# A list scheduler in the kernel's source takes over the order of every engine

## The chip, the cores and the metric

The kernel runs on one core of a Trainium2 chip. The metric is the device time of one execution in microseconds (us); several runs are taken and their median is compared. Lower is better. The engines that matter are TensorE (PE: matrix products and transposes into eight PSUM banks), VectorE (DVE), ScalarE (ACT), GpSimd (POOL), and SP, whose queue issues all of the kernel's DMAs. Each engine executes its own instructions in order, and they wait for each other through semaphores.

## The reference

Four layers are applied in turn to an activation `x` of 8 batches x 256 tokens x 512 features in fp32, with a conditioning vector `cond_2048` (8 x 512).

```python
# layer 0: conditioned RMS norm, 8 query heads on one key head (64 wide), SwiGLU MLP of 2048
h = ada_rms(x, t, ln1_w, ln1_tw); q, k = apply_rope(h @ Wq.T), apply_rope(h @ Wk.T); v = h @ Wv.T
x = x + softmax(q k^T / 8) v @ Wo.T
h = ada_rms(x, t, ln2_w, ln2_tw); x = x + (silu(h @ Wg.T) * (h @ Wu.T)) @ Wd.T
# layer 1: 16 heads of 32 with normalised q and k, a bias on the scores, gelu MLP of 2048, gates
x = x + attn(_ln(x) * (scale1 + 1) + shift1) * gamma1
x = x + (gelu_tanh((_ln(x) * (scale2 + 1) + shift2) @ Wfc1.T + bfc1) @ Wfc2.T + bfc2) * gamma2
# layer 2: 16 query heads on 4 key heads of 32, low-rank keys and values, a sparse causal mask
c_kv = h @ Wkd.T; k, v = c_kv @ Wku.T, c_kv @ Wvu.T
x = x + softmax(mask(rope(q) rope(k)^T / sqrt(32))) v @ Wo.T
# layer 3: 8 block experts of 64 -> 256 -> 64, layer norm with conditioning, silu, projection
y = gelu(xr @ W1 + b1) @ W2 + b2
x = x + silu(layernorm(y) * (1 + scale) + shift) @ out_W + out_b
```

## The kernel before

Tokens lie in 16 tiles of 128 x 512, which stay in SBUF from start to end (`x0` to `x15`), two to a batch. The stages follow each other: layer 0's attention, its MLP, layer 1's attention, its MLP, layer 2's attention, layer 3.

**Attention** (`attend`, three times). For each batch and group of four heads TensorE makes the scores into the four PSUM banks with the tag A (`scored`, L697, tiles of 32 or 64 rows). VectorE finds row maxima in A (L727; in layers 1 and 2 a custom operation that also adds a bias or mask, L743), and ACT takes Exp with row sums (L747). The probabilities are then turned with the tokens of the keys on the partitions: some by TensorE (`turned`, L783) and a copy by DVE or ACT (`copy`, L480 and L483), some by a DVE transpose of 32 x 32 blocks and a round trip through memory (four DMAs out, L549, and one back, L756: the tensors `flip`). The values are multiplied in (`weighted`, L808), the result is divided by the row sums (`divided`, L830; inverse sums go through memory as `spread`, L765 and L770), and the projection with `wo` is added to `x` (`added`, L631). The product helper L631 also makes queries, keys and values of the next batch, which `rope` (L649, L650) turns before they are transposed (L1258, L1264). Norms use statistics (L449, L450), a power on POOL, and a scaling (L468, L470); a batch's normalised tiles are transposed on TensorE (L500) or through memory (`turn`).

**MLPs** (`mlp`): products of 128 x 128 blocks, seven in place of eight by sums of blocks (Strassen), into C banks (L1024) and A banks (L1073).

**Conditions**: `cond_rows` and `modulation` (L316, L334) make scales and shifts from `cond_2048` and weights such as `wada1`.

What sets the order. `Program` calls the engines' methods through a tile framework in a given program order. Extra work (projection of the next batch, output of the last one, conditions) is kept in generators on `self.queue` and taken up between the steps of the attention by a credit of microseconds (`some`). The framework takes these instructions, tracks which tile each reads and writes, and puts them on the engines by a scheduler and cost model of its own; it also hands out the buffers of each tag (`BUFS`: four A banks, four C banks, four `p`, two `hT`, eight `wbig` and so on). Three hints in the source bend it: `tc.keep_in_program_order(...)` on modulations, on some products of values and on layer 2's first scores, and `tc.issue_after(self.last_dma)`, which queues the loads of the next layer behind the last inverse sums on SP.

Of the kernel before, what the change touches and what calls it, by code (L numbers as in the profile page):

```python
# [14 lines left out]

# [19 lines left out]
P = 128  # L35
# [3 lines left out]
KC = D // P  # L39
# [139 lines left out]

class Program:  # L180
    def __init__(self, ctx, tc, d, out):
        self.ctx, self.tc, self.nc, self.d, self.out = ctx, tc, tc.nc, d, out
        self.n = 0
        self.queue, self.credit = [], 0.0
        self.ready, self.calls = {}, 0

    def pool(self, name, psum=False):
        return self.ctx.enter_context(
            self.tc.tile_pool(
                name=name, bufs=1, reuse_waits="tile", **({"space": PSUM} if psum else {})  # L190
            )
        )

    def t(self, shape, tag, bufs=None, dtype=F32, pool=None):
        self.n += 1
        bufs = bufs or BUFS.get(tag)
        kw = {} if bufs is None else {"bufs": bufs}
        pool = pool or (
            self.psum if tag in "AC" else self.wbigp if tag == "wbig" else self.work
        )  # L200
        return pool.tile(list(shape), dtype, tag=tag, name=f"{tag}_{self.n}", **kw)
# [29 lines left out]
    def setup(self):  # L231
        nc, d = self.nc, self.d
        self.const = self.pool("const")
        self.xp = self.pool("xp")
        self.wqkvp = self.pool("wqkvp")
        self.wop = self.pool("wop")
        self.wbigp = self.pool("wbigp")
        self.work = self.pool("work")
        self.psum = self.pool("psum", psum=True)

        def c(shape, tag, **kw):
            return self.t(shape, tag, pool=self.const, **kw)
# [6 lines left out]
        self.x = [self.t([P, D], f"x{i}", pool=self.xp) for i in range(NT)]  # L249
# [11 lines left out]
        make_identity(nc, self.ident)  # L261
# [3 lines left out]
        for t in self.inv:  # L265
            nc.gpsimd.memset(t, 0.0)
        self.spread = [
            self.tc.dram_tile([32, P], F32, name=f"spread{i}") for i in range(4)
        ]
        self.n_spread = 0  # L270
        self.turns = [self.tc.dram_tile([P, KC * S], F32, name=f"turn{i}") for i in range(3)]
        self.n_turn = 0
        self.flips = [self.tc.dram_tile([P, 8 * P], F32, name=f"flip{i}") for i in range(4)]
# [94 lines left out]
    def ada_1(self):  # L368
# [11 lines left out]
        self.gammas = self.tc.dram_tile([2, B, D], F32, name="gammas")  # L380
# [202 lines left out]
    def modulate(self):  # L583

        for (name, b), entry in self.ready.items():
            hT, rows, kept, at, done = entry
            if rows is None and not done and at < math.inf:
                place, placed, _ = self.places(name, b, hT)
                for c in range(KC):
                    self.tc.keep_in_program_order(placed(c, c, place[:, c]))  # L590
# [64 lines left out]
    def attend(self, name, n_groups, hd, project, value, finish, work, key_tiles=(2, 2), biased=None,  # L655
# [29 lines left out]
        def scored(b, g):  # L685
# [3 lines left out]
            for j0 in range(0, 4, rows):  # L689
                for q in range(TB):  # L690
                    for j in range(j0, j0 + rows):
# [5 lines left out]
                        mm = nc.tensor.matmul(  # L697
# [3 lines left out]

                        if name == "attention2" and j == q == 0:
                            self.tc.keep_in_program_order(mm)
            return s

        def softmax(s, b):
# [61 lines left out]
            for c in range(nch):  # L768
                t = inverse[(self.n_spread * nch + c) % 4]
                dma = nc.sync.dma_start(  # L770
                    t, rows[c * per : (c + 1) * per, :].unsqueeze(1).to_broadcast([per, hd, S])
                )
                self.last_dma = dma.ins
# [16 lines left out]
        def weighted(b, g, pT):  # L790
# [11 lines left out]
            for c in range(nch):  # L802
                for k in range(TB):
                    mine = [n for n, (kk, q) in enumerate(pairs) if kk == k]
                    q0 = pairs[mine[0]][1]
                    for i in range(per):
                        j = c * per + i
                        mm = nc.tensor.matmul(  # L808
# [7 lines left out]
                        if j < self.in_blocks(name, b):  # L816
                            self.tc.keep_in_program_order(mm)
# [186 lines left out]
    def mlp_begin(self, name):  # L1004
        self.kept = self.tc.dram_tile([B, P, 7 * S], F32, name=name)
        self.first = self.blocked(0, self.hT)
# [213 lines left out]
    def layer0_begin(self):  # L1220
        nc = self.nc
        w = self.t([P, KC, 1536], "wqkv", pool=self.wqkvp)
        self.load(w[:, :, 0:512], "wq0T")
        self.load(w[:, :, 512:640], "wkv0T")
        wo = self.t([P, KC, D], "wo", pool=self.wop)
# [130 lines left out]
    def layer0_mlp(self):  # L1356
# [4 lines left out]
        spare = self.t([P, 4, 2, S], "wo", pool=self.wop)  # L1361
# [10 lines left out]
        with self.tc.issue_after(self.last_dma):  # L1372
            for i, tag in enumerate(("qT", "kT", "v", "qT")):
                load_down(i, tag)
            early = []
            for i, tag in ((4, "kT"), (5, "v")):
                early.append(self.t([P, 4, S], tag))
# [622 lines left out]
```

## Time and profile before

| What | Value |
|---|---|
| median of three runs | 2079.61 us (2076.65 to 2082.24) |
| the profiled execution: its span, first to last instruction | 2076.6 us, the profile's only time for it |
| mean granted TensorE clock | 0.987 |
| PE busy | 2006.0 us, 12818 matmul records |
| DVE, ACT, POOL busy | 1365.2, 748.1, 334.0 us |
| DMA | 208.91 MB, mean 101 GB/s |

The share of busy time is an average over stages with different limits. The stages in the span are: layer 0's begin and attention from 0 to 282 us, its MLP to 868, layer 1's attention to 1258, its MLP to 1650, layer 2's attention to 1935, and layer 3. A matmul's record shows its time from start to a modelled end, and records overlap; from the start of one to the start of the next is what it costs TensorE.

The profile names engines PE, PEld (loading of weights), DVE, ACT, POOL, SP; "L631" is a line of the kernel. A group `C<-wqkv,hT 128*128 128x512` writes a tile C from tiles wqkv and hT, with a matmul tile of 128 rows x 128 columns of the array and a moving operand of 128 x 512. What stands after `<-` in brackets is the engine, tile and line that ended an idle time.

### The profile page before, as it was taken

The numbers are of one execution on the slowest core, as the hardware profiler recorded it, in microseconds if no ns is written. First come the engines' busy times: TensorE is split into PE (matmuls) and PEld (weight loads), VectorE is DVE, ScalarE is ACT, GpSimd is POOL, SyncE is SP. The second block draws the span as 40 slices with busy tenths as digits, with TensorE's granted clock in tenths as the row PEclk, the third lists the DMA queues.
The fourth block names the chain that finished last, engine by engine and source line by source line (L and its number), as shares of the span: only waits on it lengthen the run. The fifth ranks groups of instructions, "written<-read, shape, count | busy, mean of one in ns | idle before, by whom it ended". The sixth has DMA issues, their size and how long they took to land.

```text
span 2076.6 us, 36333 instructions
## 1 busy us (share of the span) xinstructions
PE 2006.0 (97%) x12818; PEld 1480.9 (71%) x12818; DVE 1365.2 (66%) x4429; ACT 748.1 (36%) x2332; POOL 334.0 (16%) x372
## 2 busy tenths in 40 slices
PE   7999999999999999999999999999999989989999
PEld 4555579999999999954544447999999854445454
DVE  6867766656675555656676766776765678776544
ACT  4333421111111111136565653222222256565644
POOL 1111200000000000054544531000000021101411
PEclk9999999999999999999999999999999989999999
DMA  8543361112130010334555543233211245653411
GB/s 306 166 119 90 102 215 48 65 42 64 61 110 26 17 31 16 96 99 129 131 143 141 141 123 115 89 101 116 87 60 48 67 113 137 158 145 97 126 40 42
DMA packets 223685, 208.91 MB, mean 101 GB/s; under 512 B 83536, under 2 KB 184976, under 8 KB 223120
## 3 DMA queue, kind: packets, MB, share of 16 engines
q1 hardware_dynamic: 223504, 206.59, 34.3%
q8 instruction: 102, 1.67, 0.3%
q14 instruction: 79, 0.65, 0.1%
HBM read 135.46 MB, written 71.07 MB: 99 GB/s over the span
## 4 chain that ended last, share of the span: by engine, by line
PE 78%; DVE 7%; ACT 7%; DMA 4%; issue 2%; POOL 2%; SPq 1%; DVEq 0%; ACTq 0%; POOLq 0%
PE C L1024 29%; PE A L1073 18%; PE C L631 17%; PE A L697 3%; ACT p L747 3%; PE C L808 3%; ACT wbig L747 2%; PE C L783 2%; PE C L1887 2%; PE A L1789 1%; DMA turn<-hT 1%; PE C L1822 1%; DVE st L449 1%; DMA wbig<-in_wgT 1%; DVE n L650 1%
## 5 line engine op out<-in xcount | busy, mean ns | idle before, releaser
L1024 PE MATMUL C<-hT,wbig 128*128 128x128 f32 x3072 | 416.4, 275 | 0.0
L1024 PEld LDWEIGHTS C<-hT,wbig 128*128 128x128 f32 x3072 | 388.8, 192 | 9.0 <-issue 2.4
L631 PE MATMUL C<-wqkv,hT 128*128 128x512 f32 (+1 forms) x768 | 316.6, 553 | 0.9 <-ACT v L1516 0.4
L1073 PE MATMUL A<-wbig,p 128*128 128x256 f32 x1024 | 242.2, 379 | 0.0
L631 PEld LDWEIGHTS C<-wqkv,hT 128*128 128x128 f32 x768 | 134.0, 195 | 122.8 <-issue 108.5
L1073 PEld LDWEIGHTS A<-wbig,p 128*128 128x128 f32 x1024 | 189.7, 190 | 23.1
L1054 DVE TENSOR_TENSOR p<-p,C 128x256 f32<-128x256 f32 x192 | 79.3, 421 | 162.5 <-PE C L1024 160.8
L1044 ACT COPY p<-C 128x128 f32<-128x128 f32 x192 | 51.3, 267 | 370.3 <-PE C L1024 361.8
L1024 PE MATMUL C<-qk,wbig 128*128 128x128 f32 x1152 | 160.0, 275 | 0.0
L1024 PE MATMUL C<-ctxT,wbig 128*128 128x128 f32 x1152 | 160.0, 275 | 0.0
L457 POOL TENSOR_SCALAR r<-mv 128x2 f32<-128x2 f32 (+1 forms) x28 | 7.1, 254 | 929.0 <-DVE mv L450 929.0
L747 ACT ACTIVATE p<-p,low 128x256 f32<-128x256 f32 x256 | 127.3, 501 | 69.9 <-DVE low L743 48.4
L1024 PEld LDWEIGHTS C<-qk,wbig 128*128 128x128 f32 x1152 | 144.1, 192 | 0.0
L1024 PEld LDWEIGHTS C<-ctxT,wbig 128*128 128x128 f32 x1152 | 144.1, 192 | 0.0
L747 ACT ACTIVATE wbig<-wbig,low 128x128 f32<-128x128 f32 (+1 forms) x256 | 113.7, 448 | 78.9 <-DVE low L743 75.9
L1398 ACT ACTIVATE p<-C 128x128 f32<-128x128 f32 x64 | 17.8, 278 | 294.9 <-DVE p L1054 294.9
L1045 DVE TENSOR_TENSOR p<-p,C 128x128 f32<-128x128 f32 x192 | 55.0, 286 | 97.5 <-ACT p L1044 96.4
L631 PE MATMUL C<-wo,ctxT 128*128 128x512 f32 x224 | 103.1, 600 | 1.2 <-DVE ctxT L830 1.2
L1504 POOL TENSOR_TENSOR ss<-ss,neg_half 128x16 f32<-128x16 f32 x32 | 93.8, 2931 | 2.7
L747 ACT ACTIVATE p<-A,low 128x256 f32<-128x256 f32 x128 | 59.3, 486 | 87.0 <-DVE low L727 75.9
L697 PE MATMUL A<-kT,qT 32*128 32x256 f32 (+2 forms) x896 | 85.9, 399 | 1.4 <-ACT p L747 0.6
L697 PEld LDWEIGHTS A<-kT,qT 32*128 32x128 f32 (+1 forms) x896 | 52.4, 191 | 41.9 <-issue 29.0
(268 smaller groups left out, 3507.6 us busy)
## 6 DMA issues: line engine op xcount, KB each, us to landing
flip<-p SPq DMA_DIRECT2D x160, 128.0 KB
p<-flip SPq DMA_DIRECT2D x40, 512.0 KB
turn<-hT SPq DMA_DIRECT2D x120, 128.0 KB
flip<-wbig SPq DMA_DIRECT2D x112, 96.0 KB
wbig<-flip SPq DMA_DIRECT2D x28, 384.0 KB
hT<-turn SPq DMA_DIRECT2D x16, 512.0 KB
kept<-hT SPq DMA_DIRECT2D x16, 512.0 KB
hT<-kept SPq DMA_DIRECT2D x16, 512.0 KB
```

What stands on the lines that cost most here:

```text
L631: self.nc.tensor.matmul(out, lhsT(k), rhs(k), start=(k == 0), stop=(k == n - 1))
L697: mm = nc.tensor.matmul(s[j][:, at[q] : at[q] + wide[q]], lhsT(q), keys, start=True, stop=True,)
L747: nc.scalar.activation(out, src, AF.Exp, bias=low[:, q : q + 1], scale=sign, accum_out=tot[:, j, q : q + 1],)
L783: nc.tensor.transpose(m[:, n * P : (n + 1) * P], p[:, at[q] + k * P : at[q] + (k + 1) * P], self.ident,)
L808: mm = nc.tensor.matmul(o[i * hd : (i + 1) * hd, c * S + q0 * P : (c + 1) * S], value(got[b][1], g, j, k), weights(j, mine), start=(k == 0 ...
L1024: nc.tensor.matmul(m[:, c : c + P], w[:, k * P : (k + 1) * P], b[:, k], start=(first and k == 0), stop=(k == steps - 1), skip_group_check= ...
L1044: nc.scalar.copy(g[:, 0, :], m[:, 0:P])
L1045: nc.vector.tensor_tensor(g[:, 0, :], g[:, 0, :], m[:, P : 2 * P], ALU.add)
L1054: nc.vector.tensor_tensor(g[:, 1:3, :], g[:, 0, :].unsqueeze(1).to_broadcast([P, 2, P]), m[:, 2 * P : 4 * P].rearrange("p (i t) -> p i t", ...
L1073: nc.tensor.matmul(acc[at][:, half * S : (half + 1) * S], left, right, start=(p == 0 and half == 0), stop=(p == 3), skip_group_check=True,)
L1504: nc.gpsimd.tensor_tensor(r, r, self.neg_half[:, 0:16], ALU.pow)
L1887: nc.tensor.matmul(m[:, half * S : half * S + S], left[:, r, i, :], right[:, i, :], start=(first and i == 0), stop=(i == 1), skip_group_ch ...
```

## The change

The program is no longer handed to the framework as it is made. `Program` gets a `Recording` in place of `nc`: `rec.tensor`, `rec.vector`, `rec.scalar`, `rec.gpsimd` and `rec.sync` note each call as an `Op` with its engine, outputs and inputs, and tiles are stand-ins without a place. `Scheduler` then

- builds the graph of dependencies by exact regions of tiles (`graph`), with whole banks for the tags A and C,
- walks the recorded operations once in order, with the buffer counts of each tag, and gives every operation a place (`program_order`),
- and goes through time (`run`): at each step it takes the engine that can start the earliest. On that engine it looks at up to 40 operations whose predecessors have been issued (`choice`), works out when each could start, and takes the one that comes first in place among those that start within 5 ns of the earliest, 200 ns on TensorE. A tile gets its buffer at its first use, if the tiles that come later in place still fit (`room`, `safe`).

Times come from formulas in the source: `duration` for DVE, ACT and POOL, `transfer` for DMAs, and the class `Tensor` for TensorE, with the change of tile shape, the overlap of tiles on different parts of the array, and table loads on ACT.

`Recording.issue` then issues the operations in that order, and adds a dependency without semaphore from each to the one before it on its engine, so that the framework keeps it. All tiles are allocated once, as homes by tag and slot; the framework still sets the semaphores. The pools, `keep_in_program_order` and `issue_after` are gone. The calls that make up the computation are the same. The diff, cut to its core:

```diff
+class Unit:
+    def __getattr__(self, method):
+        def issue(*args, **kwargs):
+            self.rec.ops.append(Op(ENGINES[self.name], self.name, method, args, kwargs))
+        return issue
...
+class Recording:
+    def issue(self, ctx, tc, order):
+        nc = tc.nc
+        seq, slots = order
...
+        make_identity(nc, real(self.ident))
+        info = mybir.DependencyInfo(mybir.DependencyClass.NoSync, mybir.DependencyReason.DATA)
+        before = {}
+        for i in seq:
+            op = self.ops[i]
+            done = getattr(getattr(nc, op.unit), op.name)(
+                *[real(a) for a in op.args], **{k: real(v) for k, v in op.kwargs.items()}
+            ).ins
+            if op.engine in before:
+                tc.add_manual_dep(done, before[op.engine], info, reason="order")
+            before[op.engine] = done.name
+LATENCY = {"PE": 38, "DVE": 33, "ACT": 33, "POOL": 35, "SP": 60}
...
+class Tensor:
+    def place(self, form, t):
+        mode, part, turn, _ = form
+        first = 84 if mode != (P, P) else 55 if turn else 104
+        if mode != self.mode:
+            return max(t, self.end + 94), first
+        soon = max(self.parts.get(part, 0.0), self.last + 7)
+        t = max(t, soon)
+        return t, first if t > soon + 30 and t > self.end + 20 else 0
...
+class Scheduler:
+    WINDOW, NEAR, NEAR_PE = 40, 5, 200
...
+        def choice(e):
+            found = []
+            for at, i in waiting[e]:
+                r = room(i)
+                if r is None:
+                    continue
+                t = max(free[e], ready[i], r + LATENCY[e] if r > 0 else 0.0)
+                extra = 0
+                if e == "PE":
+                    t, extra = pe.place(cost[i], t)
+                elif e == "ACT" and cost[i][2] not in (None, table):
+                    extra = 1283
+                found.append((t, extra, at, i))
+                if len(found) >= self.WINDOW:
+                    break
+            if not found:
+                return None
+            near = min(t + extra for t, extra, _, _ in found)
+            near += self.NEAR_PE if e == "PE" else self.NEAR
+            t, extra, _, i = min((f for f in found if f[0] + f[1] <= near), key=lambda f: f[2])
+            return t, extra, i
...
+            if e == "PE":
+                end = pe.put(cost[i], t, extra)
+                free[e] = t
+            elif e == "SP":
+                landed = max(t + 1690, landed) + cost[i]
+                free[e], end = t + 360, landed + 450
+            else:
+                took, busy, needs = cost[i]
+                free[e], end = t + extra + busy, t + extra + took
...
-        pool = pool or (
-            self.psum if tag in "AC" else self.wbigp if tag == "wbig" else self.work
-        )
-        return pool.tile(list(shape), dtype, tag=tag, name=f"{tag}_{self.n}", **kw)
+        return self.nc.tile(list(shape), dtype, tag, f"{tag}_{self.n}", bufs or BUFS.get(tag, 1))
...
-                    self.tc.keep_in_program_order(placed(c, c, place[:, c]))
+                    placed(c, c, place[:, c])
...
-        with self.tc.issue_after(self.last_dma):
-            for i, tag in enumerate(("qT", "kT", "v", "qT")):
-                load_down(i, tag)
...
+        for i, tag in enumerate(("qT", "kT", "v", "qT")):
+            load_down(i, tag)
...
+    rec = Recording()
+    Program(rec, d, out).run()
+    order = Scheduler(rec).run()
     with tile.TileContext(nc) as tc:
         with ExitStack() as ctx:
-            Program(ctx, tc, d, out).run()
+            rec.issue(ctx, tc, order)
```

The order that results, as both programs show it: in layer 1 and layer 2 many groups of scores stand ahead of the value products that came before them; at the start two groups' Exp stand together on ACT, with the angles' Sin behind them; the statistics of layer 2's second batch and one of its normalised tiles stand in the tail of layer 1's MLP on VectorE.

## The prediction

> **What bounds the kernel now.** I read the page first, then the time cut by stage, then the chain, then TensorE's waits, then two stretches in order of time. The page's busy times:
>
> ```profile
> PE 2006.0 (97%) x12818; PEld 1480.9 (71%) x12818; DVE 1365.2 (66%) x4429; ACT 748.1 (36%) x2332; POOL 334.0 (16%) x372
> ```
>
> TensorE binds, but 97% hides room, since a record's time holds its waits and its pipeline. The chain in order of time (start us, us, what) gives the true pitch:
>
> ```profile
> 315.33 3.02 PE A L1073 x14
> 318.36 6.25 PE C L1024 x56
> ...
> 2059.10 13.75 PE C L631 x32
> ```
>
> So a 128-column matmul record costs 6.25/56 = 0.112 us, 256 columns 3.02/14 = 0.216, 512 columns 0.430. From start to start in the trace, a 512-column record followed by one of another tile shape takes 0.522 instead of 0.429: a change of shape costs 0.093. Matmuls on different 32-row, 32-column or 64-wide parts start 0.007 apart and overlap. I laid all 7,002 matmul instructions of the kernel's order (12,818 records: two passes each, 1,186 transposes one) end to end at these pitches, with its 406 changes of shape: 1919.0 us. The span is 2076.6, so **157.6 us are stalls**. By stage (columns: stretch, length, busy of PE, PEld, DVE, ACT, POOL, clock, DMA share, GB/s):
>
> ```profile
> 0.00:100.00 100.00, 82.04 (x440) 47.83 (x442) 71.72 (x227) 36.76 (x101) 15.65 (x37) 0.93 0.72 239
> ...
> 282.00:868.00 586.00, 586.00 (x4406) 559.71 (x4403) 362.36 (x1175) 95.36 (x285) 6.53 (x14) 1.00 0.20 61
> ...
> 868.00:950.00 82.00, 80.34 (x354) 45.90 (x353) 51.61 (x161) 32.89 (x97) 40.77 (x34) 0.94 0.38 105
> ...
> 950.00:1200.00 250.00, 248.78 (x1374) 121.74 (x1369) 170.88 (x571) 150.68 (x477) 132.78 (x115) 1.00 0.54 142
> ...
> 1650.00:1710.00 60.00, 50.58 (x270) 32.47 (x268) 42.54 (x167) 27.49 (x98) 16.67 (x18) 0.86 0.35 91
> ...
> 1710.00:1935.00 225.00, 203.29 (x1458) 107.64 (x1458) 169.93 (x722) 136.83 (x529) 41.91 (x49) 0.98 0.51 131
> ```
>
> Span less end-to-end time per stage: layer 0's start and attention (0 to 282 us) 50, its MLP -1, layer 1's attention (868 to 1258) 36, its MLP -1, layer 2's attention (1650 to 1935) 59, layer 3 and the tail 15. The two MLPs (978 us) can give nothing. Of the 158, idle gaps are 2076.6 - 2006.0 = 70.6, and a granted clock of 0.987 over the span costs 0.013 x 2076.6 = 27; the other 60 lie inside records. TensorE's longest waits (us in total, times, longest):
>
> ```profile
> PE C L316 <- DMA condT<-in_condT: 6.8, 1, 6.8
> ...
> PE C L631 <- issue: 5.8, 3, 1.9
> ...
> PE C L500 <- DVE n L470: 5.3, 2, 3.2
> ...
> PE C L334 <- DVE n L330: 3.4, 1, 3.4
> ```
>
> The first is the first load and stays. The others are single places where something was queued in an unlucky order.
>
> **The change, part by part.** Both programs have the same 7,002 matmuls, 4,429 VectorE operations (same kinds and counts) and 1,073 DMAs; only order and buffer places differ. The stages stay apart: laid end to end, the first score of layer 2 comes at 1583.9 us in the old order and 1579.8 in the new, so nothing of an MLP moves into an attention stage, and gains must come from the 158.
>
> *Packing.* The new order has 384 changes of shape, 22 fewer: 22 x 0.093 = 2.0. Laid end to end it is 1915.4: **-3.6** (ends -4 and -3, since this is counted).
>
> *Tables on ACT at the start.* The old order alternates Exp and Sin:
>
> ```profile
> 33.12 1.28 ACT L1215 ACT_TABLE_LOAD   x1
> ...
> 34.84 1.28 ACT L747 ACT_TABLE_LOAD   x1
> ...
> 36.72 1.28 ACT L1217 ACT_TABLE_LOAD   x1
> ...
> 38.52 1.28 ACT L747 ACT_TABLE_LOAD   x1
> ```
>
> The new order runs all eight Exp of two groups before the next Sin. Table loads go from 22 to 16: four fewer here (5.1 us of ACT), two fewer where layer 0's MLP begins, worth nothing because TensorE is 100% busy there and nothing of it waits. The loads at 38.52 end in a 2.08 us gap of TensorE at 40.44, and the clock is 0.5 from 41.1 to 47.9 (3.4 us lost). I take **-4**; ends 0 (the transposes wait for VectorE's reductions instead) and -8.5 (all 5.1 and the clock).
>
> *Conditions at the start.* The second product of layer 1's conditions has its transposes some 28 rows of scores and transposes later in the new order, where the old one has three scores between. That covers the 3.4 us wait (L334) and its half clock, 3.4 us at 0.5, 1.7 lost: up to -5.1. New wait: the first product now stands ahead of the first scores, right behind the transposes that ran at 24.3 us, so the rest of the first transposes and the scores behind it would wait for two 1 MB loads of wada1. About 6.3 MB are issued up to them; at the 311 GB/s moved from 24 to 48 us that is 20.3 us, beside a first use at about 25. Cover 4 us, gone if the loads share the rate with the 5 MB behind them: +5. I take **-4**; ends -5.1 and +5.
>
> *SP's queue.* The old order held later loads behind the last spread of the attention. Now wada2 (1 MB) and three blocks of wdT (1.5 MB) are issued ahead of the first spread: 2.5 MB/311 GB/s = 8.0 us later for the inverse sums. Behind them wait VectorE's division (L830), then the product with wo; in the old trace that wait was 1.2 us in all, and the new order has two batches' transposes and the condition products in front. I take **0**; ends 0 and +8. The four parts of a flip now interleave with the next group's; each is one SP issue of about 0.4 us, and SP waits 36.5 us for flips already without TensorE waiting more than 2.4 us for them. Other start and attention waits of layer 0 (50 less those named): **-2**, ends -5 and +5.
>
> *Layer 2's beginning* (start us, us, engine, line; idle before):
>
> ```profile
> 1668.22 2.59 PE L697 MATMUL A<-kT,qT 32*128 32x128 f32 x16
> 1672.90 0.69 PE L500 MATMUL C<-ident,n 128*128 128x128 f32 x2 [2.10 <-DVE n L470]
> 1676.76 1.54 PE L500 MATMUL C<-ident,n 128*128 128x128 f32 x6 [3.16 <-DVE n L470]
> ```
>
> The old order puts batch 1's statistics and both normalised tiles behind the first group's softmax on VectorE. The new one has the statistics and the first tile in the MLP's tail, where VectorE has gaps, and puts ten further scores ahead of the second tile's first transpose. The 5.3 us go; the clock at 0.5 from 1672.6 to 1682.9 (5.1 lost) may go with them. Next late is the softmax itself. I take **-8**; ends -10.4 and +3 (its A banks are not read in time).
>
> *Scores ahead of their predecessors' products.* Counting complete groups of value products (L808) behind each group of scores, scores lead by 1.97 groups in layer 1 and 2.91 in layer 2 before; 2.75 and 3.22 after (about 25 and 10 of 32 groups move by one). In layer 2 a group of value products is 0.86 us, so VectorE's reductions start that much sooner; 1710 to 1935 has some 42 us of stalls, three of them the 1.9 us gaps shown as issue. 10 groups x 0.86 = 8.6. I take **-8**; ends -22 (half of the 42) and +10. In layer 1, 950 to 1200 is 99.5% busy with 14 us of stalls in six batches, so there is little to win; a score that comes before its bank A is read now holds the products behind it. I take **+2** there and **-5** for the stage's two ends (12 and 10 us of stalls), together **-3**; ends -15 and +15.
>
> At layer 1's beginning the clock is 0.50 from 911.5 to 921.7 although TensorE was busy 3.48 of the 3.50 us before it, in a run of 32-row scores; the new order keeps that run. So by the rows the 5.1 us lost there stay. The Trainium skill, "TensorE: Matmul & The Clock Gate", Part 1 (the HAM clock gate), puts a return to half rate down to an idle window of about 3.4 us; by that rule the stretch before 911.5 would not have triggered it, and an order without gaps would win all of it. By the rule the sum would be some 5 us lower; I go by the row.
>
> *Layer 3.* Its table loads stay (Gelu and Silu still alternate), the order differs little: **0**; ends -3 and +4.
>
> Sum: -3.6 - 4 - 4 + 0 - 2 - 8 - 8 - 3 + 0 = -32.6, so a span of 2044. The profiled span, 2076.6, is 3.0 below the median of the three runs (2079.6); the same distance puts the new median at **2047 us** (-1.6%).
>
> **Rivals.**
> *Early scores block TensorE (slower).* TensorE takes its order strictly. A group of scores needs its four A banks, which VectorE empties in eight reductions at about 0.5 us each (0.42 and 0.08): 4.0 us. Counting work of TensorE between a wait and the newest matmul it depends on, 184 waits now have under 1.5 us of cover, against 154 before. If each of the 35 moved groups waits 1.9 us more (half the reductions), that is +67 and the time 2114. It decides from 0.9 us per group (33/35). For: that count. Against: VectorE is 63 to 76% busy in these stages.
> *The order changes nothing that matters (no change).* Stalls are chains of ACT and VectorE whose lengths stay, and each gap reappears one group on: only packing and half of the table term remain, 2079.6 - 3.6 - 2 = 2074. Against: the named gaps have one cause each.
> *Loads crowd the start.* The new waits for wada1 and the spread come to +13 in place of -4: 2064.
> *Most stalls of attention go.* Half of layers 1 and 2 (48), 12 at the start, 3.6 packing: 2016.
>
> **How the numbers follow.** Forecast 0.47, most stalls go 0.15, loads crowd 0.07, no change 0.08, blocking 0.23. The forecast's own range is 2025 to 2066. For 8 in 10, the low end reaches past the strong case to 2008 (with the tables' end of -8.5 too), the high end to 2098, half-way into blocking. About 0.3% (6 us) is what a measurement tells from none: faster takes the first three, 0.69; no change gives 0.07 to same and 0.01 to slower, which with blocking is 0.24.
>
> **What would show it.** Right: two table loads fewer around 33 to 40 us and no 2 us gap there; no 3 us gap at layer 2's first L500 transposes; mean clock above 0.99; PE busy plus gaps near 2044; the MLPs unchanged at 586 and 392. Wrong: new gaps before the scores (A banks) released by VectorE, layer 1's attention longer than 390 us, or a first condition product waiting for wada1.

## The result: 0.7% slower, and where the time went

The changed kernel takes 2094.0 us (median of 4 runs, 2090.9 to 2099.5), beside 2080.4 for the kernel before (4 runs): a ratio of 1.0071, 95% interval 1.0053 to 1.009. The profiled span is 2092.7 us; before it was 2076.6, so 16.1 us more have to be found. The forecast was 2047, faster. The direction was wrong; the time lies near the slow end of the stated range (2008 to 2098).

The page of the changed kernel, its line of busy times:

```profile
PE 1995.5 (95%) x12818; PEld 1486.6 (71%) x12818; DVE 1410.0 (67%) x4429; ACT 742.9 (36%) x2326; POOL 332.4 (16%) x372
```

TensorE's records are 10.5 us shorter, its gaps 26.6 longer (97.2 in place of 70.6). By stage (stretch, length, busy of PE, PEld, DVE, ACT, POOL, clock, DMA share, GB/s):

```profile
0.00:100.00 100.00, 77.60 (x451) 44.20 (x452) 81.45 (x248) 32.37 (x99) 19.20 (x42) 0.98 0.78 260
282.00:868.00 586.00, 584.61 (x4366) 552.88 (x4365) 378.84 (x1153) 94.82 (x293) 6.50 (x14) 1.00 0.18 54
868.00:950.00 82.00, 81.73 (x417) 55.50 (x416) 58.92 (x177) 28.54 (x78) 32.00 (x29) 1.00 0.45 121
950.00:1200.00 250.00, 244.40 (x1384) 123.11 (x1383) 173.11 (x573) 153.79 (x489) 132.79 (x114) 1.00 0.52 139
1650.00:1710.00 60.00, 58.62 (x299) 40.97 (x297) 45.69 (x164) 27.00 (x93) 14.69 (x16) 0.91 0.40 99
1710.00:1935.00 225.00, 199.20 (x1420) 107.84 (x1420) 169.14 (x728) 132.75 (x516) 27.47 (x35) 0.95 0.52 133
```

Layer 1's beginning now runs at full clock. (From layer 1 on, the changed kernel's stages lie some 16 us later than those of the kernel before, so rows of the same times do not hold quite the same work.) The waits of TensorE (us in total, times, longest) say what was paid for it. All operations now have line 320, so one goes by tiles; `kept_flip` is the tensor `flip` of the kernel before, `kept_spread` is `spread`, `kept_turn` is `turn`:

```profile
PE C L320 <- DMA p<-kept_flip: 33.9, 11, 10.3
PE C L320 <- DMA wbig<-kept_flip: 15.6, 9, 3.2
PE C L320 <- ACT wbig L320: 8.1, 8, 4.1
PE C L320 <- DMA condT<-in_condT: 6.9, 1, 6.9
PE C L320 <- DVE n L320: 4.5, 7, 1.7
...
PE A L320 <- ACT p L320: 0.4, 1, 0.4
```

The first two lines are value products that wait for the read-back of a flip: 49.5 us, where the kernel before had 2.4. 22.9 of them are four waits between 100 and 282 us. The last line is what the strongest rival stood on, scores blocked by a bank A: 0.4 us.

The prediction's ledger (the order laid end to end at the trace's pitches, and the rest as stalls), in us. Each layer's column ends at the layer's last value product and begins where the column before it ends, so it holds the MLP that comes before its attention; "rest" is what follows layer 2's last value product, layer 3 above all:

| kernel | end to end | layer 0 | layer 1 | layer 2 | rest | span |
|---|---|---|---|---|---|---|
| before | 1919.0 | 49.8 | 34.2 | 58.9 | 14.7 | 2076.6 |
| changed | 1915.4 | 69.7 | 30.6 | 58.6 | 18.4 | 2092.7 |
| difference | -3.6 | +19.9 | -3.6 | -0.3 | +3.7 | +16.1 |

So the loss is layer 0's, and layer 2's gain is missing. SyncE's queue in time (start us, us, what) shows how layer 0 came about. The kernel before, one group:

```profile
174.32 1.76 SPq L549 DMA_DIRECT2D flip<-p  x4
176.18 0.56 SPq L765 DMA_DIRECT2D spread<-invT  x1
178.09 0.34 SPq L756 DMA_DIRECT2D p<-flip  x1
178.52 1.07 SPq L770 DMA_DIRECT2D wqkv<-spread  x2
```

The changed kernel, the end of a group:

```profile
179.57 2.20 SPq L320 DMA_DIRECT2D kept_flip<-p  x2
186.05 1.07 SPq L320 DMA_DIRECT2D wqkv<-kept_spread  x2
187.28 0.88 SPq L320 DMA_DIRECT2D p<-kept_flip  x1
```

and what TensorE did with that read-back:

```profile
195.90 3.63 PE L320 MATMUL C<-p,kT 128*64 128x256 f32 x16 [4.41 <-DMA p<-kept_flip]
```

The stretches (columns as above) in which spread loads run, in the kernel before. The DMA share is the busy share of 16 DMA engines, here called rings:

```profile
181.00:182.00 1.00, 1.00 (x3) 0.38 (x2) 0.53 (x1) 0.00 (x0) 0.00 (x0) 1.00 0.17 64
...
185.00:186.00 1.00, 1.00 (x4) 0.46 (x3) 0.00 (x0) 0.00 (x0) 0.00 (x0) 1.00 0.14 48
```

and in the changed one. In the last two rows TensorE waits; in the last of all the spread loads are through, and what runs is the rest of the read-back:

```profile
184.00:185.00 1.00, 1.00 (x4) 0.46 (x3) 0.00 (x0) 0.00 (x0) 0.00 (x0) 1.00 0.13 47
...
193.00:194.00 1.00, 0.00 (x0) 0.00 (x0) 0.29 (x2) 0.00 (x0) 0.54 (x2) 1.00 0.14 48
194.00:195.00 1.00, 0.00 (x0) 0.00 (x0) 0.00 (x0) 0.00 (x0) 0.50 (x2) 1.00 0.13 53
```

The `spread` loads bring a group's inverse sums, two loads of 128 KB, each from 2 rows to 2 x 64 partitions. While they run the DMA share is 0.13 to 0.14, that is 2.1 to 2.2 of 16 rings, at some 47 GB/s: 256 KB take over 5 us. The old order issues the read-back first and the spread loads fall into a quiet stretch. The new one issues them first; its model puts every transfer on all 16 rings, so it counts some 0.4 us for each of them. The read-back is split over all rings, and if two of them are busy it is whole only when those are through: issued at 187.28, it releases TensorE at 195.9. The trace's DMA packets show this. The read-back has 128 packets of 4096 bytes. 112 of them start by 191.7 us, up to 16 at a time; the other 16, two rings' share, start from 193.95 to 195.14, two at a time, when the spread loads' packets are gone. The four read-backs that make up the 22.9 us all have this gap before their last 16 packets (2.3 to 2.7 us), all stand behind two spread loads, and took 8.1 to 9.0 us from issue to TensorE. A fifth in layer 0, at 93.94 with no spread load just ahead of it, took 3.2. This reading was put to the test.

### The profile page after: what moved, and what is told of

Read it like the earlier page. It is cut to its first block, busy times and chain, and to the rows that moved or that the text cites. A ratio compares the mean times of both kernels' runs of the same rounds, so it can differ in the third digit from the quotient of the medians.

```text
span 2092.7 us, 36267 instructions
## 1 busy us (share of the span) xinstructions
PE 1995.5 (95%) x12818; PEld 1486.6 (71%) x12818; DVE 1410.0 (67%) x4429; ACT 742.9 (36%) x2326; POOL 332.4 (16%) x372
## 3 DMA queue, kind: packets, MB, share of 16 engines
q1 hardware_dynamic: 223504, 206.59, 34.2%
## 5 line engine op out<-in xcount | busy, mean ns | idle before, releaser
L320 DVE TENSOR_TENSOR p<-p,C 128x128 f32<-128x128 f32 (+1 forms) x832 | 259.2, 316 | 218.4 <-PE C L320 140.8
L320 ACT COPY p<-C 128x128 f32<-128x128 f32 (+1 forms) x288 | 105.6, 370 | 399.3 <-PE C L320 379.3
L320 DVE TENSOR_TENSOR p<-p 128x384 f32<-128x384 f32 (+1 forms) x576 | 173.5, 318 | 63.8 <-ACT p L320 52.9
L320 ACT ACTIVATE p<-p,low 128x256 f32<-128x256 f32 x256 | 127.0, 498 | 74.2 <-DVE low L320 54.3
L320 ACT ACTIVATE wbig<-wbig,low 128x256 f32<-128x256 f32 (+1 forms) x256 | 113.1, 444 | 34.1 <-DVE low L320 32.0
L320 ACT ACTIVATE p<-C,vec 128x128 f32<-128x128 f32 x64 | 23.5, 367 | 169.8 <-DVE p L320 169.8
```

The source lines that it names most:

```text
L320: done = getattr(getattr(nc, op.unit), op.name)(*[real(a) for a in op.args], **{k: real(v) for k, v in op.kwargs.items()}).ins
```

## The experiments

Labels run e1 to e19 ("the third run" in an expectation is e3, and so on; there is no e5). No kernel leaves work out. Those without another note start from the changed kernel. The expectations name five theories. A: the scheduler's model makes every transfer too short. B: early scores block TensorE. D: the spread loads go ahead of the read-backs and hold a few rings. E: SP falls behind its model in layers 1 and 2. F: loads for layer 2, freed from their place, crowd layer 1's last read-backs.

| kernel | us | ratio to before, 95% | layer 0 | layer 1 | layer 2 | waits for flips |
|---|---|---|---|---|---|---|
| e1 spread loads behind the read-back | 2084.3 | 1.0009 to 1.0028 | 58.9 | 25.3 | 63.9 | 23.9 |
| e2 read-back 5.5 us later in the model | 2136.1 | 1.0257 to 1.0287 | 60.1 | 74.0 | 54.3 | 15.5 |
| e3 all spread loads cut into rows | 2071.9 | 0.9957 to 0.998 | 38.4 | 39.1 | 60.8 | 36.4 |
| e4 NEAR_PE 0 | 2251.3 | 1.0806 to 1.0839 | 89.0 | 128.9 | 69.3 | 81.4 |
| e6 before, all cut into rows | 2118.6 | 1.0174 to 1.0208 | 44.3 | 55.7 | 80.9 | 19.0 |
| e7 e3, 480 ns an issue | 2059.3 | 0.9898 to 0.9927 | 38.1 | 39.3 | 46.9 | 31.5 |
| e8 rings in the model | 2088.4 | 1.0026 to 1.0056 | 67.1 | 41.7 | 46.6 | 34.1 |
| e9 layer 0's loads cut | 2063.0 | 0.9913 to 0.9942 | 38.7 | 30.9 | 56.2 | 21.7 |
| e10 e9, 480 ns | 2062.9 | 0.9901 to 0.9933 | 38.7 | 32.3 | 58.4 | 24.5 |
| e11 before, layer 0's loads cut | 2067.6 | 0.9931 to 0.996 | 42.6 | 33.5 | 58.5 | 0.8 |
| e12 e9, 600 ns | 2053.8 | 0.9862 to 0.9891 | 39.2 | 32.9 | 48.6 | 23.9 |
| e13 e9, flips in turn | 2182.9 | 1.0478 to 1.0521 | 41.4 | 60.0 | 129.6 | 54.3 |
| e14 e9, layer 2's loads held | 2062.7 | 0.9882 to 0.9941 | 39.2 | 26.9 | 61.2 | 21.5 |
| e15 e12, rings in the model | 2046.7 | 0.9814 to 0.9867 | 38.9 | 32.1 | 39.6 | 11.7 |
| e16 e15, layer 2's loads held | 2045.2 | 0.9811 to 0.9859 | 39.3 | 33.1 | 42.8 | 13.4 |
| e17 e12, layer 2's loads held | 2055.1 | 0.9864 to 0.9904 | 38.5 | 34.2 | 51.3 | 22.4 |
| e18 600 ns and rings, no load cut | 2053.6 | 0.9859 to 0.9907 | 54.5 | 28.9 | 38.9 | 12.3 |
| e19 e9, rings, 360 ns | 2065.0 | 0.9926 to 0.9956 | 40.6 | 42.9 | 45.0 | 25.5 |

The layers' columns are stalls of the profiled execution; the last column is TensorE's waits for a flip's read-back in all.

**e1: the order on SP undone for one pair of transfers.**

```diff
+        back = None
+        for i, op in enumerate(ops):
+            if op.engine != "SP":
+                continue
+            name = op.ins[0].tensor.name
+            if "flip" in name:
+                back = i
+            if "spread" in name and back is not None:
+                self.before[i].setdefault(back, False)
         self.after = [[] for _ in range(n)]
```

> One order-only edge: in SP's order the loads of the inverse sums (kept_spread to SBUF) stand behind the read-back of the same group's flip, as in the kernel before; TensorE's order in layer 0 stays that of the changed kernel, row for row. Theory D (two loads of inverse sums go ahead of the read-back and hold a few DMA rings for about 5 us: the trace of the changed kernel has 1024-byte packets at 0.14 of 16 rings from 187 to 195 us while the read-back's last 4096-byte packets wait): TensorE's waits for p<-kept_flip between 100 and 282 us fall from 22.9 us to under 5, the time from 2094 to about 2070 to 2076 (layer 0 gives back 18, layers 1 and 2 some 3). Theory A (the scheduler's latency of a transfer is too short, whatever stands ahead of it): the waits stay above 15 us and the time is 2085 to 2096. Theory B (early scores block TensorE): no change, 2090 to 2097.

The waits for p<-kept_flip between 100 and 282 us went from 22.9 us to none, as theory D had it. But layer 0 gave back 10.8 us, not 18. All waits of TensorE in that stretch:

```profile
PE A L320 <- ACT p L320: 7.1, 1, 7.1
PE C L320 <- DVE x L320: 5.7, 1, 5.7
PE A L320 <- DVE v L320: 2.1, 1, 2.1
PE C L320 <- DVE n L320: 0.3, 1, 0.3
```

The first two stand behind another transfer, the read-back `hT<-kept_turn` of normalised tiles turned through memory, which ScalarE and VectorE wait for before they read the banks. In e1 it is what SP issues next after the spread loads:

```profile
218.53 1.05 SPq L320 DMA_DIRECT2D wqkv<-kept_spread  x2
...
219.69 1.63 SPq L320 DMA_DIRECT2D hT<-kept_turn  x1
...
229.30 0.91 ACT L320 ACTIVATE hT<-hT,mod 128x256 f32<-128x256 f32 x2 [8.57 <-DMA hT<-kept_turn]
```

It too came 9.6 us after its issue, at 219.69 and again at 270.04. Only the third wait (2.1 us) is for the sums themselves. So the flips' read-backs were helped and another one took their place behind the two loads.

**e3 and e9: the loads cut, so that they run on more rings.** In e9 only where a load has two rows (layer 0), in e3 everywhere:

```diff
-                nc.sync.dma_start(
-                    t, rows[c * per : (c + 1) * per, :].unsqueeze(1).to_broadcast([per, hd, S])
-                )
+                for k in range(per):
+                    nc.sync.dma_start(
+                        t[k * hd : (k + 1) * hd, :],
+                        rows[c * per + k : c * per + k + 1, :].to_broadcast([hd, S]),
+                    )
```

> The loads of the inverse sums are cut into one load for each row of sums (64 or 32 partitions from one row of 256), the same bytes and packets; the outermost dimension of a load is then the 64 or 32 copies and no longer the 2 or 4 rows. Theory D, if the rings are shared out by the outermost dimension: the stretch of 1024-byte packets at 0.14 busy goes, the same 128 KB go at 0.8 or more, read-backs in layer 0 reach TensorE within 5 us of their issue in place of 8 to 9, TensorE's waits for flips between 100 and 282 us fall from 22.9 to under 8 and the time to 2070 to 2080, though SP issues 32 and up to 192 loads more (some 0.55 us each on SP). Theory A: the read-backs take as long as now and the time is 2090 to 2105.

> Only the loads of layer 0, whose load has 2 rows of sums (two loads of 128 KB a group), are cut into rows; layers 1 and 2 keep one load of 4 rows. TensorE's instructions stand as in the changed kernel (384 changes of shape, 1915.4 us end to end). Theory D: all of the difference between the third run and the changed kernel lies in layer 0: waits for p<-kept_flip between 100 and 282 us under 3 us in place of 22.9, time 2065 to 2074. If the gain of the third run came from its other order in layers 1 and 2: 2080 or more.

In e9 the instructions of TensorE, VectorE, ScalarE and GpSimd stand exactly in the changed kernel's order; SyncE's alone differ. On SP the spread loads still go ahead of the read-back (the group below has them issued from 172.99, the read-back at 175.48). A stretch of spread loads in e9, and then all its waits of TensorE between 100 and 282 us:

```profile
175.00:176.00 1.00, 1.00 (x3) 0.38 (x2) 0.00 (x0) 0.00 (x0) 0.00 (x0) 1.00 0.31 105
```

```profile
PE C L320 <- DMA p<-kept_flip: 1.7, 1, 1.7
PE C L320 <- DVE n L320: 0.3, 1, 0.3
PE A L320 <- ACT p L320: 0.2, 1, 0.2
```

The loads now run at 105 GB/s in place of 47, with mostly three to seven of their packets under way at a time in place of two: 256 KB are through in 2.8 us. SP issues one load of 64 KB every 0.6 us, which is about that rate. The waits fall from 22.9 to 1.7 us, layer 0 from 69.7 to 38.7 us of stalls, and the kernel from 2094.0 to 2063.0: 0.7% faster than the kernel before, with the same order on four engines. Layers 1 and 2 stay within 3 us of the changed kernel's. That settles layer 0: its loss is the spread loads on two rings, ahead of the read-back. e3's further cuts in layers 1 and 2 (192 more issues on SP) lost 9 us again, most of them in layer 1 (39.1 against 30.9).

**e6 and e11: the same cuts in the kernel before.** All loads in e6, layer 0's in e11.

> The kernel before with the loads of the inverse sums cut into rows, as in the third run; it tells how much of that run's gain (2071.9 against 2094) is owed to the new order's use of the rings and how much any order would get. Theory D: in the kernel before the spread loads stand behind the read-back (issued at 178.52 us, the read-back at 178.09) and their 5.5 us at 0.14 busy fall into a quiet stretch, and flips cost TensorE 2.4 us in all; so at most 3 us to win: 2075 to 2081. If instead shorter spread loads help any order (the division by the sums comes earlier): 2060 to 2070, and the order itself is still the loser.

> The kernel before with layer 0's loads alone cut into rows; beside the 2063.0 of the same edit in the changed kernel it tells what the new order is worth once the two-ring loads are gone. From the run with all loads cut: layer 0 stalls 44.3 us in place of 49.8, so theory D gives 2072 to 2077, and the new order is then worth 9 to 14 us; if layer 0's gain was that edit's in any order: 2055 to 2066, and the new order is worth nothing.

e6 missed on the slow side: layer 0 gained 5.5 us, layers 1 and 2 lost 43.5. Its longest waits of TensorE are:

```profile
PE C L631 <- issue: 20.3, 5, 4.3
PE C L810 <- DMA p<-flip: 17.5, 5, 6.2
```

e11, whose TensorE order is that of the kernel before in all but 23 places, gained 12 us, more than expected; 7 of them are layer 0's. So the two-ring loads cost the old order something too, only less. With them gone on both sides, the new order is worth 2067.6 - 2063.0 = 4.6 us as it stands (the intervals of the two ratios overlap a little), about a seventh of the 32.6 forecast.

**e2 and e8: later transfers in the scheduler's model alone.**

```diff
 e2
                 free[e], end = t + 360, landed + 450
+                if "flip" in ops[i].ins[0].tensor.name:
+                    end += 5500
 e8
-    return size / length * (9 + 0.0365 * length) / 16
+    rings = min(16, in_.ap[0][1]) if any(step == 0 for step, _ in in_.ap) else 16
+    return size / length * (9 + 0.0365 * length) / rings
```

> The scheduler's model alone is changed: a flip's read-back counts as visible 5.5 us later (in layer 0 of the changed kernel it reached TensorE 8 to 9 us after its issue, in the model about 3.5). SP's greedy choice stays, so the spread loads still go ahead of the read-backs. Theory A: TensorE's waits for flips (49.5 us in the changed kernel) fall under 10 and the time to 2045 to 2065. Theory D: the round trip itself stays 8 to 9 us in layer 0, but the order now covers it, so the waits fall as well; D alone does not forbid 2055 to 2075. Theory B: value products later still and scores earlier still, so more scores wait for banks: slower, 2095 to 2115, with new waits of A on VectorE or ACT.

> Nothing on the chip is cut: the scheduler's model alone is changed, a load with a repeated dimension is counted on as many rings as its outermost dimension has rows (2 or 4) and not on 16. Theory D with the model at fault: the order covers the long loads, TensorE's waits for flips between 100 and 282 us fall under 8 us and the time to 2070 to 2080. Theory D with the rings at fault (the greedy choice on SP still sends the spread loads first, and a later read-back only moves the products, as in the second run, where 5.5 us more in the model gave 2136): 2085 to 2110.

e2 answers theory A, that a longer latency by itself mends the order: layer 0's waits for flips do go (0.9 us), but the products' order is pulled so far apart that layer 1 stalls 74.0 us, with waits for ctxT (18.3 us in 11 in that layer), the tile that the value products' results go into, and 14.6 us for flips still. 5.5 us was far too much there: where TensorE waited for a read-back in layers 1 and 2 of the changed kernel, it came 3.3 to 6.3 us after its issue, against some 3.5 in the model. e8 hardly helps layer 0 (67.1), but layer 2 falls from 58.6 to 46.6.

**e4 and e13: the rival, and the interleaved flips.** e4 sets NEAR_PE to 0. e13 is e9 with an edge from each read-back to the next flip's writes:

```diff
+            if "flip" in op.ins[0].tensor.name:
+                back = i
+            if "flip" in op.outs[0].tensor.name and back is not None:
+                self.before[i].setdefault(back, False)
```

> NEAR_PE is 0 in place of 200: of TensorE's instructions the one that the model starts first is always taken, the recorded order decides only between equals. Theory B (matmuls taken too early block TensorE): more of them, so slower than the changed kernel, 2105 to 2130, with longer waits before scores. Theories A and D: the flip's round trip is the same, so its waits stay near 50 us and the time within 15 us of 2094.

> Layer 0's loads cut into rows, and an order-only edge that keeps a flip's four writes behind the read-back of the flip before, as in the kernel before: no interleaving of flips on SP. If interleaving is what makes the read-backs of layers 1 and 2 late: waits for flips fall from 21.7 to under 8 us; but the order loses packing (1933 us end to end in place of 1915, 405 changes of shape), so the time is 2055 to 2075. If interleaving costs nothing, as the prediction had it: waits for flips as in the cut kernel (20 us), and the loss of packing shows: 2075 to 2090.

e4 is slower than every theory said. Its waits for flips are 81.4 us, 17.1 of them in layer 0 between 100 and 282 us; waits for a bank A are 5.6 us in all. Taking matmuls earlier costs, then, but hardly by the mechanism of the rival. e13 fell out of both expectations: the waits for flips rose from 21.7 to 54.3 us. It doesn't tell what interleaving costs, since the whole order is another (1933 us end to end), and it is no way to mend it.

**e7, e10, e12 and e18, e19: the model's numbers.** 360 ns for an issue on SP becomes 480 or 600; e12 and e19 part the two numbers that e18 has together on the uncut kernel.

> Rows as in the third run, and the scheduler counts 480 ns for an issue on SP in place of 360 (the changed kernel's trace: 0.50 us mean for a part of a flip, 0.56 for a sum's write, 0.59 for a turned block). Theory E (in layers 1 and 2 the read-backs are late because SP falls behind its model, and value products are placed too early): the 36 us of waits for flips left in the third run fall to under 18 and the time to 2050 to 2062. If SP's own time is not what makes them late (the four writes of one flip are spread over 4 us, and each has to land): 2066 to 2076, waits for flips over 25 us.

> Layer 0's loads cut into rows (2063.0 with that alone) and 480 ns for an issue on SP in the scheduler's model. The seventh run's rows in layers 1 and 2 gave those layers' SP 3 issues more per group; without them theory E (SP falls behind its model in layers 1 and 2) gives 2045 to 2057, with under 12 us of TensorE's waits for flips in place of 21.7. If SP's time in the model does not matter: 2060 to 2066.

> As the run with 480 ns, with 600. Theory E with the traces' mean of some 0.5 us: too much now, 2050 to 2065; if more latency in the model always costs (5.5 us on the read-backs cost 42 us): above 2066.

> The scheduler's model alone (600 ns for an issue on SP, rings of the loads with a repeated dimension), no load cut: the same transfers as in the changed kernel. If the model can order around the two-ring loads of layer 0: 2045 to 2062. If layer 0 needs the loads cut, because SP still sends them ahead of the read-backs (theory D with the rings at fault): layer 0 keeps 60 to 70 us of stalls by 282 us and the time is 2066 to 2080.

> Layer 0's loads in rows and rings in the model, 360 ns for an issue. It parts the two changes of the model in the 2046.65 kernel. If the rings alone give layer 2's gain (the eighth run, with 360 ns, had 44 us there): 2046 to 2056, layer 2's stalls 40 to 46. If 600 ns is needed as well: 2056 to 2066, layer 2's stalls above 48.

e7's time fits theory E, its waits for flips (31.5) don't. e10 gains nothing over e9, e12 gains 9 us, 7.6 of them in layer 2. e18 changes no transfer's size or number and is at 2053.6, 40 us below the changed kernel and 25 below the kernel before: the loss can be undone in the model alone, though layer 0 keeps 54.5 us where the cut loads give 39. e19 says that rings in the model bring layer 2 down (45.0 with 360 ns) and spoil layer 1 (42.9 in place of 30.9). How large the effect of one number is can't be read from one pair, since every edit of the model reshuffles the whole order, and layer 1 lies anywhere from 27 to 43 us in the kernels built on e9, e13 aside. Differences under some 6 us between two orders are left without a cause here.

**e14 and e17: layer 2's loads held.** The change also drops a line that kept three loads (wq2T, wkdT, wkvuT) behind the last spread load of layer 1. In the changed kernel they go at 1218.6 us, ahead of the last read-back, and the stretch behind them looks guilty:

```profile
1220.00:1230.00 10.00, 8.35 (x38) 3.64 (x36) 6.27 (x14) 3.73 (x12) 0.94 (x2) 1.00 0.91 278
```

The edge puts them behind that read-back (backs is the list of read-backs, the 40th is layer 1's last):

```diff
+        for i in loads:
+            self.before[i].setdefault(backs[39], False)
```

> The twelfth kernel (2053.8) with one order-only edge: layer 2's three loads wq2T, wkdT and wkvuT (1.4 MB) stand on SP behind the last read-back of layer 1, as in the kernel before; TensorE's order is the same. Theory F (these loads, freed from their place, fill the rings ahead of layer 1's last read-backs: DMA share 0.91 from 1220 to 1230 us in the changed kernel, then a 5 us gap and half clock): the 17.8 us of stalls between 1200 and 1258 us fall to about 10, as in the kernel before (10.1), and the time to 2043 to 2048. If the wait there is the round trip's own: 2051 to 2056.

> Layer 0's loads in rows, and the same edge, with 360 ns for an issue as in the changed kernel. So both causes found are gone and the scheduler's model is as it was. Theory F: 2063.0 less 6 to 8, so 2054 to 2058; stalls between 1200 and 1258 us about 9 in place of 15.9. Otherwise 2060 to 2066.

In e17, whose TensorE order is e12's, theory F fell: the time is the same (2055.1 against 2053.8), and the wait between 1190 and 1258 us is there without the loads. e12, then e17:

```profile
PE C L320 <- DMA p<-kept_flip: 6.6, 1, 6.6
```

```profile
PE C L320 <- DMA p<-kept_flip: 5.8, 2, 4.1
```

In e14 the stalls from 1200 to 1258 us did fall as F has it (9.1 us in place of e9's 15.9, but layer 1 ends inside this stretch; its whole column fell by 4.0). Its TensorE order differs from e9's in 16 places around 1211 to 1220 us. Layer 2 lost 5 us, and the time is e9's. So the loads aren't shown to cost anything; why the last groups of layer 1 wait stays open.

**e15 and e16: together.**

> The twelfth kernel, and in the model a load with a repeated dimension counts on as many rings as its outermost dimension (4 in layers 1 and 2). Theory E for layer 2 (the predicted 16 us were there, and late read-backs ate them): with this in the model the eighth run had 44 us of stalls between 1650 and 1925 us, against 57.5 in the kernel before and 55.6 in the changed one; so layer 2 falls from 49.4 to 40 to 45 and the time to 2044 to 2050. If the eighth run's layer 2 was a lucky order: 2051 to 2060.

> All of them: layer 0's loads in rows, 600 ns for an issue, rings in the model, layer 2's loads held. If theories D, E and F add up: 2036 to 2043. If they overlap: 2043 to 2052.

e15's longest waits are

```profile
PE C L320 <- DMA p<-kept_flip: 9.5, 4, 6.3
PE C L320 <- DMA condT<-in_condT: 7.2, 1, 7.2
PE C L320 <- ACT wbig L320: 5.5, 9, 1.1
PE C L320 <- DVE n L320: 4.4, 6, 2.1
```

Layer 2's waits for flips, 12.9 us in e12, are down to 2.2 us there, and layer 2 stalls 39.6 us. e15 beats the kernel before by 1.6%, the changed one by 47 us. e16, with the same TensorE order, is no different, which is a second answer to theory F.

## Why the prediction was wrong

*SP's queue, put at 0, is the step that failed.* It counted the loads that go ahead of the first spread, and of the flips it said that each part "is one SP issue of about 0.4 us, and SP waits 36.5 us for flips already without TensorE waiting more than 2.4 us for them". In layer 0 the short wait was a property of the old issue order (read-back, then spread loads), which the change gives up. In its place stand 49.5 us of waits, and +18.9 us of stalls from 100 us to the end of layer 0 alone, outside the term's own end of +8. The part that it did price stayed small: up to 100 us VectorE waited 2.35 us for a spread load, and TensorE 1.48 for the division behind it. In layers 1 and 2 that issue order isn't the reason: e1 restores it and keeps 23.9 us of waits there, against 25.5. In layer 2 the read-backs came 3.3 to 4.2 us after their issue, near the model's 3.5, so most of the lateness there lies before the issue; e15 and e18, with later transfers in the model, bring it down, but what holds the issue was not taken apart. The evidence was in the trace of before: shares of 0.11 to 0.17 from 181 to 187 us, behind the spread loads of the group shown, and the model of the changed source that divides each transfer by 16. A page bears on it that the prediction didn't use: the Trainium skill, "DMA: Bandwidth & Descriptors", section "Why a DMA increments its semaphore by 16 and not by 1", has a transfer run on the largest number of engines up to 16 that divides the outermost dimension (not of size 1) of both sides. By it the two-row loads run on 2 and the cut ones on 16. The runs agree with the 2 (0.13 to 0.14 of 16, two packets at a time). Of the cut loads they show more than 2 (a share of 0.31), but not 16, since SP issues them too slowly to fill the rings.

*Scores ahead of their predecessors, layer 2 (-8), and layer 2's beginning (-8).* Together -16; the changed kernel got 0.3. Taken from the same place in the stage (16 us later in the changed kernel), the first 60 us stall 11.8 us in place of 18.7: both gaps at the L500 transposes went, -6.9, nearly as said. The half clock that "may go with them" did not go: it is 0.51 from 1687.6 to 1698.0. The rest of the layer stalls 46.8 in place of 40.2, +6.6 where -8 was said; 15.6 us of flips' waits stand in it. e15 shows that the gain was there to be had: with read-backs on time the layer stalls 39.6 us, 19.3 under the kernel before. That these waits ate it is shown as far as e15 and e18 go, both with other orders too.

*Layer 1, -3: measured -3.6,* by other parts than said. At the beginning it won 9.2 us, with the half clock after 911.5 us. The prediction had the new order keep the run of 32-row scores there; it cuts it into 16 and 12 records with two of 512 columns between, and the clock stays 1.00. So whether the row or the rule had that clock right was not decided there. But the changed kernel has the same again at layer 2's beginning: TensorE is busy 3.59 of the 3.60 us before 1687.6, in a run of 32-row scores and transposes, and the clock is 0.51 for the next 10.4. By the records there is no idle window there either, so the row, not the rule, was the better guide. The end lost 4.5 us.

*Tables -4, conditions -4, other waits of layer 0 -2.* Table loads fell from 22 to 16 as counted, but the gap stays, released by VectorE, the term's end of 0. The conditions' 3.4 us wait went, and new ones of about its size came, for n and mv, not for wada1's loads. TensorE in the changed kernel:

```profile
30.00 1.50 PE L320 MATMUL C<-wbig,scondT 128*32 128x256 f32 x24 [1.67 <-DVE n L320]
...
43.33 0.66 PE L320 MATMUL C<-ident,p 128*128 128x128 f32 x4 [2.27 <-DVE p L320]
...
58.53 0.63 PE L320 MATMUL C<-ident,qk 128*128 128x128 f32 x4 [2.15 <-DVE mv L320]
```

Stalls up to 100 us are 33.2 us, before 32.2, and 29.2 in e9: -3 at best in place of -8. From there to the layer's end e9 has 9.5 in place of 17.6, -8 where -2 was said. That e9's layer 0 comes near the -10 of the sum (-11) is luck.

*Packing, -3.6,* is exact, as it was counted. *Layer 3, 0:* +3.7, within its end of +4.

*The rivals.* Blocking by banks had the sign right and the mechanism wrong: 0.4 us of waits for A. "Loads crowd the start" named DMA, at the first 100 us; of that, only the 1.48 us above were there. No rival named the transfer that a later instruction overtakes.

The sum of the terms, -32.6, is close to what e15 reaches (2042.2 against 2076.6 in the profiled spans, -34.4: packing -5.2, layer 0 -10.9, layer 1 -2.1, layer 2 -19.3, rest +3.1). That it comes so close is partly luck: e15 has layer 0's loads cut, which alone gave the kernel before 7.2 us in layer 0 (e11) and which the prediction did not price, and the parts at the start and in layer 1 came by other ways than said. Layer 2's part is the one that e15 supports, an order whose transfers arrive on time.

## What to carry to other kernels

When a scheduler takes over a DMA queue, ask of every transfer on the critical round trip which other transfers may now overtake it, and how many rings those use: here two loads of 128 KB with an outermost dimension of 2 made whatever read-back was issued next 5 us late, flips in the changed kernel and turned tiles in e1. A wait that is short in the old trace may be short only because of the old issue order; it is no evidence for a new one. And before a model's latencies are raised, find which transfer is slow: 5.5 us on the wrong ones cost 42 us, the right two numbers won 40.

## What the runs showed of the hardware

Two loads of 128 KB from two rows each held the share of the rings at 0.13 to 0.14 for over 5 us, and a read-back of 512 KB issued behind them took 8.6 us to release TensorE (187.28 to 195.9 us). In the same layer, without such loads just ahead, one took 3.2 us, and in the other layers they took 3.3 to 6.3. And a gap costs more than itself. The changed kernel's longest:

```profile
250.00:255.00 5.00, 5.00 (x32) 3.66 (x30) 2.62 (x11) 1.70 (x4) 2.37 (x4) 1.00 0.41 117
255.00:260.80 5.80, 0.52 (x2) 0.00 (x0) 2.41 (x5) 0.33 (x1) 1.99 (x5) 1.00 0.28 86
260.80:271.00 10.20, 5.16 (x22) 3.37 (x23) 0.94 (x3) 0.40 (x1) 0.00 (x0) 0.50 0.65 210
```

5.3 us idle, and then the clock at 0.50 for 10.2 us, in which TensorE worked 5.2 us at half rate: some 2.6 us more for a gap of 10.3. The Trainium skill, "TensorE: Matmul & The Clock Gate", Part 1 (the HAM clock gate), lets the rate halve after an idle window of about 3.4 us. This gap agrees; the half clock from 1687.6 us, with TensorE busy 3.59 of the 3.60 us before it, does not.
